# Outputs of the first layer's experts: stored by expert and gathered per token, or scattered to their tokens' rows and loaded

## The chip, the cores and the metric

The kernel runs on one core of a Trainium2 chip. A core has TensorE (PE; its weight loads are shown apart as PEld), VectorE (DVE), ScalarE (ACT), GpSimd (POOL) and SyncE (SP), and 16 DMA engines that all issuing engines share. The metric is the time of one execution in microseconds (us); of several executions the median is taken. All data are float32.

## The reference, cut to what matters

A graph transformer of two layers works on 3125 tokens with 256 numbers each. Layer 0 adds a graph attention and a linear attention to the tokens and then a mixture of eight experts, of which each token uses two. Layer 1 adds a graph convolution, another linear attention and eight dense experts.

```python
def _L0_ffn_ref(x, gate_w, gate_b, W1, b1, W2, b2):
    probs = softmax(xf @ gate_w + gate_b)
    top2_vals, top2_idx = top_k(probs, 2)
    cw = zeros((N, 8)).at[arange(N)[:, None], top2_idx].add(top2_vals)
    for w1, bb1, w2, bb2, we in zip(W1, b1, W2, b2, cw.T):
        h = gelu(xf @ w1 + bb1)
        y = h @ w2 + bb2
        acc = acc + we[:, None] * y
...
x = x + _L0_ffn_ref(_layernorm(x), ...)
xn = _layernorm(x)
x = x + _L1_gnn_ref(xn, edge_index, weight, bias) + _L1_mix_ref(xn, ...)
x = x + _L1_ffn_ref(_layernorm(x), ...)
```

## The kernel before

The tokens lie in 25 tiles of 128 rows (the last holds 53), resident as `X`. The experts of layer 0 take three steps.

*Dispatch* (`dispatch`, called for groups of up to four token tiles, interleaved with layer 0's other work). The tokens are normalised into `hd`, the gate's logits are compared, and each token gets two slots: an expert has 3328 slots in the table `tok` in device memory, filled in the order in which its tokens come. `slot` keeps the two slot numbers of each token (`slotF` as floats). GpSimd writes each token's normalised row to both slots with indirect transfers (L1172, two per token tile, 50 in all). `clear` has zeroed the table earlier, in layer 0's first part, so that unused slots read as zero rows.

*Expert tiles* (`tiles_of_experts`). A tile is 256 slots of one expert. Tiles 0 to 7 are the first of each expert; for the others `table_of_tiles`, made on DVE after the last dispatch, holds the expert and the row of each tile, and, since an output table `yex` is ordered by tile, new values of `slot` that point into `yex`. 28 tiles always run, four more stand in an `If` (L1412) that this input doesn't enter. SP loads per tile its rows (`hr`, L1354), two weights of 512 KB and a bias (`load`, rings of three). TensorE transposes `hr` (`turned`, copied by DVE to `hTe`), forms `mm` (four groups, gelu on ACT), then `acc`; DVE adds the bias into `yo` (L1394) and ACT's queue stores `yo` to `yex` as plain rows (L1395). Between the tiles SP also loads layer 1's dense experts (`fW`), three pieces of 256 KB after every third tile.

*Entry to layer 1.* The 25 token tiles go in seven groups (`ENT`: 2, 3, 4, 4, 4, 4, 4). `fetch_y` gathers for a group both outputs of each of its tokens from `yex` into `ye` (L1459, two indirect transfers per token tile, 50 in all; ring of three groups). `add_y` (L1463) adds them to `X` with their gates (L1469) and takes the mean and variance; the last tile of a group asks for the third group after it. `norm_y` normalises and transposes, `product_y` forms the rows that the graph convolution will gather and stores them group by group to `xtab` (L1498, SP), and `keys_values` forms keys and values of the linear attention. A loop (L1547 to L1562) takes the tiles in order, with the additions four tiles ahead and 18 of the 25 key steps inside. After it GpSimd gathers neighbours from `xtab` (L263), and pairs of layer 1 follow.

The order on each engine is set by the framework's scheduler; each engine runs its own list in order, and waits in front of an instruction hold up what stands behind it on that engine. Transfers go through three queues: SP's and ACT's (plain transfers), and GpSimd's (indirect ones).

Of the kernel before, what the change touches and what calls it, by code (L numbers as in the profile page):

```python
# [8 lines left out]
F32 = mybir.dt.float32  # L9
I32 = mybir.dt.int32  # L10
AF = mybir.ActivationFunctionType
ALU = mybir.AluOpType
AX = mybir.AxisListType

N, E, D = 3125, 50000, 256
P = 125
NT = N // P
# [5 lines left out]
NE = 8  # L23
# [32 lines left out]
def bc(ap, axis, n):  # L56

    a = ap.unsqueeze(axis)
    shape = list(a.shape)
    shape[axis] = n  # L60
    return a.to_broadcast(shape)
# [3 lines left out]
Q = 128  # L65
LAST = N - (NT - 1) * Q
NPAD = NT * Q
QB = 108
# [7 lines left out]
ME = 256  # L76
# [101 lines left out]
def fast_path(ctx: ExitStack, tc: tile.TileContext, i, out, ident, flag, X):  # L178
# [37 lines left out]
    def cols_of(name):  # L216
        return cols[:, _COLS[name][0]:_COLS[name][1]]
# [10 lines left out]
    def rows(t):  # L228
        return LAST if t == NT - 1 else Q
# [17 lines left out]
    def normed(dst, x, mv, rs, j):  # L247
        nc.vector.tensor_scalar(dst, x, mv[:, j, 0:1], rs[:, j:j + 1], op0=ALU.subtract, op1=ALU.mult)
# [78 lines left out]
    slotF = const.tile([Q, 2, NT], F32, name="slotF", tag="slotF")  # L327
    tok = dram.tile([NE * ST, D], F32, name="tok", tag="tok")
    yex = dram.tile([MT * ME, D], F32, name="yex", tag="yex")
    Mall = const.tile([Q, NCH, 4], F32, name="Mall", tag="Mall")  # L330
# [4 lines left out]
    with ExitStack() as l0:  # L335
# [14 lines left out]
        marks = dram.tile([QB * Q + NPAD, 4], F32, name="marks", tag="marks")  # L350
        zero = g0.tile([Q, Q], F32, name="zero", tag="zero")
        nc.vector.memset(zero, 0.0)
# [50 lines left out]
        def quads_of_edges():  # L403
# [23 lines left out]
            for k in range(8):  # L427
                a = k * SEGM
                if k:
# [6 lines left out]
            nc.gpsimd.dma_start(marks[0:QB * Q, :].rearrange("(p a r) c -> p a (r c)", p=QB, a=4),  # L436
                                bc(zero[0:QB, :], 1, 4))
            yield
# [231 lines left out]
        def clear(e):  # L670
            with queued():
                nc.vector.memset(zero, 0.0)
            nc.sync.dma_start(tok[e * ST:(e + 1) * ST, :].rearrange("(p r) (h c) -> p (r h) c", p=Q, h=2),
                              bc(zero, 1, 2 * ST // Q))
            if e == NE - 1:
                nc.sync.dma_start(xtab[NPAD:NPAD + 1, :].rearrange("o (h c) -> o h c", h=2), bc(zero[0:1, :], 1, 2))
                a = (MT - 4) * ME
                nc.sync.dma_start(yex[a:MT * ME, :].rearrange("(p r) (h c) -> p (r h) c", p=Q, h=2),
                                  bc(zero, 1, 8 * ME // Q))

# [435 lines left out]
        def dispatch(t0, n):  # L1116
# [3 lines left out]
            yield  # L1120
            hd = g0.tile([Q, 4, D], F32, name="hd", tag=f"m{t0 // 4 % 2}")
            pg = ps("seg", [Q, n, NE])
            for j in range(n):
                normed(hd[:, j, :], xs[:, j, :], mv, rs, j)
            yield
# [41 lines left out]
            nc.vector.tensor_reduce(sf[:, 1, :], sel, AX.X, ALU.max)  # L1167
            nc.vector.tensor_copy(slot[:, :, t0:t0 + n], sf)  # L1168
            for j in range(n):
                r = rows(t0 + j)  # L1170
                for k in range(2):
                    put = nc.gpsimd.indirect_dma_start(  # L1172
                        out=tok[:, :], out_offset=bass.IndirectOffsetOnAxis(ap=slot[0:r, k, t0 + j:t0 + j + 1], axis=0),
                        in_=hd[0:r, j, :], in_offset=None)
                    tc.add_to_no_dep_group("tok", put.ins)
                    tc.declare_no_dep(put.ins, group="tok", reason="no two tokens have the same row of an expert")
# [97 lines left out]
    with ExitStack() as l0e:  # L1274
# [6 lines left out]
        restI = ew.tile([Q, 1], I32, name="restI", tag="restI", bufs=1)  # L1281
        b1 = ew.tile([Q, MR, HB], F32, name="b1", tag="b1", bufs=1)
        be = cols_of("e_b1").rearrange("p (e f) -> p f e", f=HB)

        def table_of_tiles():

            def tmp(name, shape, dt=F32):
                return ew.tile([Q] + shape, dt, name=name, tag=name, bufs=1)
# [25 lines left out]
            nc.vector.tensor_tensor(pick, eoh, bc(start, 1, MR), ALU.mult)  # L1314
            row = tmp("row", [MR])
            nc.vector.tensor_reduce(row, pick, AX.X, ALU.add)
# [3 lines left out]
            for f in range(HB):  # L1320
                nc.vector.tensor_tensor(pick, eoh, bc(be[:, f, :], 1, MR), ALU.mult)
                nc.vector.tensor_reduce(b1[:, :, f], pick, AX.X, ALU.add)
            yield

            thr, off = tmp("thr", [NE, 2]), tmp("off", [NE, 2])
            nc.vector.tensor_copy(thr[:, :, 0], first)
            nc.vector.tensor_scalar(thr[:, :, 1], first, float(ME), None, op0=ALU.add)
            nc.vector.scalar_tensor_tensor(off[:, :, 0], eidx, -float(ME), first, op0=ALU.mult, op1=ALU.add)
            nc.vector.tensor_scalar(off[:, :, 1], start, float(ME - NE * ME), None, op0=ALU.add)
            inc = tmp("inc", [2 * NE])  # L1330
            off = off.rearrange("p e s -> p (e s)")
            nc.vector.tensor_copy(inc, off)
            nc.vector.tensor_tensor(inc[:, 1:2 * NE], off[:, 1:2 * NE], off[:, 0:2 * NE - 1], ALU.subtract)
            sp = tmp("sp", [2 * NT, 2 * NE])
            sl = slotF.rearrange("p k t -> p (k t)")
            nc.vector.tensor_tensor(sp, bc(sl, 2, 2 * NE), bc(thr.rearrange("p e s -> p (e s)"), 1, 2 * NT), ALU.is_ge)
            nc.vector.tensor_tensor(sp, sp, bc(inc, 1, 2 * NT), ALU.mult)
            back = tmp("back", [2 * NT])
            nc.vector.tensor_reduce(back, sp, AX.X, ALU.add)
            nc.vector.tensor_tensor(back, sl, back, ALU.subtract)  # L1340
            nc.vector.tensor_copy(slot.rearrange("p k t -> p (k t)"), back)
            yield

        def load(k):
# [3 lines left out]
            else:  # L1348
# [3 lines left out]
                src = tok[bass.ds(rr, ME), :]  # L1352
            hr = ew.tile([Q, 2, D], F32, name="hr", tag="hr", bufs=3)
            nc.sync.dma_start(hr, src.rearrange("(j p) c -> p j c", p=Q))  # L1354
# [19 lines left out]
        def tiles_of_experts(k0, k1):  # L1374
# [4 lines left out]
            for k in range(k0, k1):  # L1379
                w1, w2, _, b2 = loaded.pop(k)  # L1380
                gT = ew.tile([Q, HB, ME], F32, name="egT", tag="egT")
# [12 lines left out]
                nc.vector.tensor_tensor(yo, py, bc(b2, 1, 2), ALU.add)  # L1394
                nc.scalar.dma_start(yex[k * ME:(k + 1) * ME, :].rearrange("(j p) c -> p j c", p=Q), yo)  # L1395
                if k + 3 < k1:
# [55 lines left out]
    def fetch_y(g):  # L1452
        if g < len(ENT):
            t0, n = ENT[g]
            yes[g] = wk.tile([Q, 8, D], F32, name="ye", tag="gt1", bufs=3)
            for j in range(n):
                r = rows(t0 + j)
                for k in range(2):
                    nc.gpsimd.indirect_dma_start(  # L1459
                        out=yes[g][0:r, 2 * j + k, :], out_offset=None, in_=yex[:, :],  # L1460
                        in_offset=bass.IndirectOffsetOnAxis(ap=slot[0:r, k, t0 + j:t0 + j + 1], axis=0))

# [1017 lines left out]
```

## Time and profile before

| | |
|---|---|
| median of 5 executions | 2500.42 us (2498.88 to 2501.15) |
| profiled execution | 2501.07 us |
| its span | 2499.3 us |
| mean granted clock of TensorE | 0.963 |
| busy: PE, DVE, ACT, POOL | 2284.5, 1437.6, 1034.7, 1182.6 us |
| transfers | 229.92 MB, mean 92 GB/s |

The profile shows one execution. A line of it names the source line, the engine, the operation and the tiles as out<-in; the clock is the share of full speed that the throttle granted to TensorE. Where a helper issues the instructions, all have the helper's line (L260 for products, L263 for gathers), and are told apart by their tiles. "idle before, releaser" is the time in which the engine waited just before an instruction, and what ended the wait. A transfer has two times: that of its issue on a queue, and that until it has landed; the landing is known for a part of the transfers only.

Among the costliest groups, in busy us, are the gathers of layer 0 (L263 from `table`, 509.6) and of layer 1 (L263 from `xtab`, 436.8), both on POOL, the products of the dense and other experts on PE, and, each about 50 us on POOL, the gathers of L1459 and the scatters of L1172.

### The profile page before, as it was taken

To read this page: it belongs to the slowest core of one execution; us is meant where nothing else is said; L and a number is where in the kernel's file an instruction comes from. 1 tells how busy PE (TensorE), PEld (TensorE's weight loads), DVE (VectorE), ACT (ScalarE), POOL (GpSimd) and SP (SyncE) were. 2 spreads that over 40 slices of the span, in tenths; PEclk is the share of its full clock that TensorE was granted. 3 is DMA by queue.
4 is the path that set the end of the run, shared out by engine and by line. 5 is a ranking of instruction groups with operands and counts; after the bars stand their busy time and mean duration, and the time that the engine had idled before them with its cause. 6 is when DMAs were issued, how large, how long until landed. Compare 5 with 4: busy or idle time off the path is not lost. (4 is left out here: it accounts for less than half of the span.)

```text
span 2499.3 us, 27694 instructions
## 1 busy us (share of the span) xinstructions
PE 2284.5 (91%) x9288; PEld 1628.4 (65%) x9288; DVE 1437.6 (58%) x3426; ACT 1034.7 (41%) x2012; POOL 1182.6 (47%) x1250
## 2 busy tenths in 40 slices
PE   3886799999999989999899699969799999999998
PEld 3664567776677856778566588846466665656665
DVE  3475656887778977689544621247555554444331
ACT  2724235635447364383654322236243333333332
POOL 2445776726677347630022300043666766767700
PEclk8998999999999999999999799989799999999999
DMA  7103132413234131120111388622322333333300
GB/s 223 38 12 91 46 84 54 127 56 103 64 104 130 37 104 50 48 66 13 37 60 60 119 292 287 225 94 80 93 84 86 106 91 101 100 92 99 102 13 8
DMA packets 187748, 229.92 MB, mean 92 GB/s; under 512 B 25743, under 2 KB 153527, under 8 KB 187595
## 3 DMA queue, kind: packets, MB, share of 16 engines
q0 software_dynamic: 45184, 106.92, 15.0%
q1 hardware_dynamic: 131557, 111.19, 14.2%
q10 hardware_dynamic: 10854, 9.92, 1.3%
q8 instruction: 77, 1.26, 0.2%
q14 instruction: 76, 0.62, 0.1%
HBM read 169.27 MB, written 58.67 MB: 91 GB/s over the span
## 5 line engine op out<-in xcount | busy, mean ns | idle before, releaser
L263 POOL DMA_INDIRECT gt<-table,srcI x432 | 509.6, 1180 | 210.6 <-issue 119.5
L263 POOL DMA_INDIRECT gt<-xtab,src x432 | 436.8, 1011 | 224.8 <-issue 109.7
L260 PE MATMUL mm<-hT,w 128*128 128x512 f32 (+3 forms) x896 | 365.0, 546 | 7.7 <-ACT gT L975 5.1
L260 PE MATMUL acc<-w,gT 128*128 128x256 f32 (+1 forms) x1600 | 365.9, 384 | 0.1
L260 PEld LDWEIGHTS acc<-w,gT 128*128 128x128 f32 (+1 forms) x1600 | 298.6, 189 | 48.8 <-issue 3.4
L1662 ACT ACTIVATE fh<-mm,bn_b,bn_s 128x512 f32<-128x512 f32 (+2 forms) x224 | 162.0, 723 | 349.0 <-PE mm L260 348.9
L975 ACT ACTIVATE gT<-mm,cols 128x512 f32<-128x512 f32 (+3 forms) x224 | 139.8, 632 | 268.1 <-PE mm L260 266.0
L260 PEld LDWEIGHTS mm<-hT,w 128*128 128x128 f32 x896 | 163.8, 192 | 132.9 <-issue 87.2
L316 DVE SCALAR_TENSOR_TENSOR X<-acc,rw,X 128x256 f32<-128x256 f32 x200 | 94.9, 482 | 217.3 <-PE acc L260 216.9
L260 PE MATMUL mm<-wqkv,hT 128*128 128x256 f32 x800 | 205.6, 391 | 8.5 <-ACT K L849 5.3
L260 PE MATMUL acc<-fw_f_Wo,fh 128*128 128x256 f32 (+1 forms) x800 | 197.7, 385 | 0.5 <-DVE X L316 0.3
L260 PE MATMUL mm<-fh,fw_f_W 128*128 128x512 f32 (+2 forms) x448 | 187.9, 549 | 2.1
L260 PE MATMUL mm<-xc,fw_f_W 128*128 128x512 f32 (+2 forms) x448 | 185.1, 543 | 0.0
L260 PEld LDWEIGHTS acc<-fw_f_Wo,fh 128*128 128x128 f32 (+1 forms) x800 | 142.8, 187 | 54.9 <-ACT fh L1662 12.0
L260 PEld LDWEIGHTS mm<-wqkv,hT 128*128 128x128 f32 x800 | 143.7, 194 | 32.8 <-ACT K L849 9.1
L1459 POOL DMA_INDIRECT ye<-yex,slot x50 | 50.7, 1013 | 239.3 <-DVE oh L270 224.3
L260 PEld LDWEIGHTS mm<-fh,fw_f_W 128*128 128x128 f32 x448 | 81.1, 189 | 87.7 <-issue 39.9
L729 DVE TENSOR_TENSOR vals<-m,w 128x2080 f32<-128x2080 f32 x54 | 124.9, 2313 | 19.0 <-ACT w L724 18.9
L260 PEld LDWEIGHTS mm<-xc,fw_f_W 128*128 128x128 f32 x448 | 85.0, 192 | 58.5 <-issue 40.0
L260 PE MATMUL acc<-M,qT 128*128 128x256 f32 x400 | 105.1, 407 | 12.8 <-ACT qT L945 10.5
L263 POOL DMA_INDIRECT es<-etab,at x54 | 59.8, 1108 | 119.3 <-DVE at L374 98.9
L1172 POOL DMA_INDIRECT tok<-hd,slot x50 | 50.2, 1005 | 125.3 <-DVE slot L1168 86.5
(464 smaller groups left out, 3868.0 us busy)
## 6 DMA issues: line engine op xcount, KB each, us to landing
ew<-in_e_W SPq DMA_DIRECT2D x56, 512.0 KB, 4.7
tok<-zero SPq DMA_DIRECT2D x8, 3328.0 KB, 14.0
w<-in_W SPq DMA_DIRECT2D x8, 1024.0 KB, 11.5
hr<-tok SPq DMA_DIRECT2D x28, 256.0 KB, 5.3
yex<-yo ACTq DMA_DIRECT2D x28, 256.0 KB, 5.1
gt<-table,srcI POOLq DMA_INDIRECT x432, 2.5
gt<-xtab,src POOLq DMA_INDIRECT x432, 2.8
fw_f_W<-in_f_W SPq DMA_DIRECT2D x16, 256.0 KB, 2.7
```

The lines of the kernel that those rows point to most:

```text
L260: nc.tensor.matmul(pm, a, b, start=(k == 0), stop=(k == len(lhs) - 1))
L263: nc.gpsimd.indirect_dma_start(out=dst, out_offset=None, in_=tab[:, :], in_offset=bass.IndirectOffsetOnAxis(ap=idx[:, b:b + 1], axis=0))
L316: nc.vector.scalar_tensor_tensor(X[0:r, t, :], py, cw, X[0:r, t, :], op0=ALU.mult, op1=ALU.add)
L729: nc.vector.tensor_tensor(v.rearrange("p j (h f) -> p j h f", f=65), bc(m[:, h0 - b0:h0 - b0 + k, 4:69], 2, 4), bc(w[:, h0 - b0:h0 - b0 + ...
L975: nc.scalar.activation(gT[:, f, 0:w], pm, AF.Gelu, bias=col("b1", l * NF + f))
L1172: put = nc.gpsimd.indirect_dma_start(out=tok[:, :], out_offset=bass.IndirectOffsetOnAxis(ap=slot[0:r, k, t0 + j:t0 + j + 1], axis=0), in_= ...
L1459: nc.gpsimd.indirect_dma_start(out=yes[g][0:r, 2 * j + k, :], out_offset=None, in_=yex[:, :], in_offset=bass.IndirectOffsetOnAxis(ap=slot[ ...
L1662: nc.scalar.activation(hn[:, a, 0:w], pm, AF.Relu, bias=bn[s][1][:, c:c + 1], scale=bn[s][0][:, c:c + 1])
```

## The change

A row of `tok` gets two numbers more: the token's number plus one, and its first slot plus a constant `NONE`, both written into `hd` at dispatch. An expert tile thus knows for each of its rows whose token it holds, and whether this is the token's first or second slot. From that DVE makes a row number of a new table `y2`: the first outputs of all tokens in order, then the second ones, then rows of their own for empty slots. GpSimd scatters the tile's two halves there, instead of the plain store on ACT's queue. `fetch_y` becomes two plain loads per group on SP, one for the first outputs and one for the second (a third piece where the last tile has 53 rows). The part of `table_of_tiles` that turned slots into rows of `yex`, and the clearing of `yex`, are gone.

```diff
@@ -325,8 +325,11 @@
     first = const.tile([Q, NE], F32, name="first", tag="first")
     nc.gpsimd.iota(first, pattern=[[ST, NE]], base=0, channel_multiplier=0, allow_small_or_imprecise_dtypes=True)
     slotF = const.tile([Q, 2, NT], F32, name="slotF", tag="slotF")
-    tok = dram.tile([NE * ST, D], F32, name="tok", tag="tok")
-    yex = dram.tile([MT * ME, D], F32, name="yex", tag="yex")
+
+    tok = dram.tile([NE * ST, D + 2], F32, name="tok", tag="tok")
+
+    NONE = 2 * NPAD + 1
+    y2 = dram.tile([3 * NPAD + NE * ST, D], F32, name="y2", tag="y2")
     Mall = const.tile([Q, NCH, 4], F32, name="Mall", tag="Mall")
     closed = {}
     xtab = dram.tile([NPAD + 1, D], F32, name="xtab", tag="xtab")
@@ -348,7 +351,7 @@
         SEGM = 24 * SEG
         etab = dram.tile([8 * SEGM], F32, name="etab", tag="etab")
         marks = dram.tile([QB * Q + NPAD, 4], F32, name="marks", tag="marks")
-        zero = g0.tile([Q, Q], F32, name="zero", tag="zero")
+        zero = g0.tile([Q, Q + 1], F32, name="zero", tag="zero")
         nc.vector.memset(zero, 0.0)
         oks = const.tile([Q, 8], F32, name="oks", tag="oks")
         nc.vector.memset(oks, 1.0)
@@ -434,7 +437,7 @@
                 a += 3 * W * (P1 - q)
                 nc.gpsimd.dma_start(etab[a:(k + 1) * SEGM].rearrange("(p j) -> p j", p=1), zero[0:1, 0:(k + 1) * SEGM - a])
             nc.gpsimd.dma_start(marks[0:QB * Q, :].rearrange("(p a r) c -> p a (r c)", p=QB, a=4),
-                                bc(zero[0:QB, :], 1, 4))
+                                bc(zero[0:QB, 0:Q], 1, 4))
             yield
             bF = tmp("bF", [RB], tag="vs", p=1)
             nc.vector.tensor_copy(bF, bI)
@@ -670,13 +673,11 @@
         def clear(e):
             with queued():
                 nc.vector.memset(zero, 0.0)
-            nc.sync.dma_start(tok[e * ST:(e + 1) * ST, :].rearrange("(p r) (h c) -> p (r h) c", p=Q, h=2),
-                              bc(zero, 1, 2 * ST // Q))
+            n = ST // Q * (D + 2) // (Q + 1)
+            nc.sync.dma_start(tok[e * ST:(e + 1) * ST, :].rearrange("(p r) c -> p (r c)", p=Q)
+                              .rearrange("p (n c) -> p n c", n=n), bc(zero, 1, n))
             if e == NE - 1:
-                nc.sync.dma_start(xtab[NPAD:NPAD + 1, :].rearrange("o (h c) -> o h c", h=2), bc(zero[0:1, :], 1, 2))
-                a = (MT - 4) * ME
-                nc.sync.dma_start(yex[a:MT * ME, :].rearrange("(p r) (h c) -> p (r h) c", p=Q, h=2),
-                                  bc(zero, 1, 8 * ME // Q))
+                nc.sync.dma_start(xtab[NPAD:NPAD + 1, :].rearrange("o (h c) -> o h c", h=2), bc(zero[0:1, 0:Q], 1, 2))
 
         m2 = []
 
@@ -1118,10 +1119,12 @@
             xs = X[:, t0:t0 + n, :]
             mv, rs = ln_stats(xs, n)
             yield
-            hd = g0.tile([Q, 4, D], F32, name="hd", tag=f"m{t0 // 4 % 2}")
+            hd = g0.tile([Q, 4, D + 2], F32, name="hd", tag=f"m{t0 // 4 % 2}")
+            nc.gpsimd.iota(hd[:, 0:n, D], pattern=[[Q, n]], base=t0 * Q + 1, channel_multiplier=1,
+                           allow_small_or_imprecise_dtypes=True)
             pg = ps("seg", [Q, n, NE])
             for j in range(n):
-                normed(hd[:, j, :], xs[:, j, :], mv, rs, j)
+                normed(hd[:, j, 0:D], xs[:, j, :], mv, rs, j)
             yield
             for j in range(n):
                 pt = transposed(hd[:, j, :])
@@ -1166,6 +1169,7 @@
             nc.vector.tensor_tensor(sel, took, at, ALU.mult)
             nc.vector.tensor_reduce(sf[:, 1, :], sel, AX.X, ALU.max)
             nc.vector.tensor_copy(slot[:, :, t0:t0 + n], sf)
+            nc.vector.tensor_scalar(hd[:, 0:n, D + 1], sf[:, 0, :], float(NONE), None, op0=ALU.add)
             for j in range(n):
                 r = rows(t0 + j)
                 for k in range(2):
@@ -1280,6 +1284,9 @@
         rowI = ew.tile([Q, MR], I32, name="rowI", tag="rowI", bufs=1)
         restI = ew.tile([Q, 1], I32, name="restI", tag="restI", bufs=1)
         b1 = ew.tile([Q, MR, HB], F32, name="b1", tag="b1", bufs=1)
+        rowF = ew.tile([Q, MR], F32, name="rowF", tag="rowF", bufs=1)
+        nth2 = ew.tile([Q, 2], F32, name="nth2", tag="nth2", bufs=1)
+        nc.gpsimd.iota(nth2, pattern=[[Q, 2]], base=0, channel_multiplier=1, allow_small_or_imprecise_dtypes=True)
         be = cols_of("e_b1").rearrange("p (e f) -> p f e", f=HB)
 
         def table_of_tiles():
@@ -1312,7 +1319,7 @@
             nc.vector.scalar_tensor_tensor(start, tiles, -float(ME), first, op0=ALU.mult, op1=ALU.add)
             pick = tmp("pick", [MR, NE])
             nc.vector.tensor_tensor(pick, eoh, bc(start, 1, MR), ALU.mult)
-            row = tmp("row", [MR])
+            row = rowF
             nc.vector.tensor_reduce(row, pick, AX.X, ALU.add)
             nc.vector.scalar_tensor_tensor(row, nth, float(ME), row, op0=ALU.mult, op1=ALU.add)
             nc.vector.tensor_scalar(row, row, float(ME), float(NE * ST - ME), op0=ALU.add, op1=ALU.min)
@@ -1320,25 +1327,6 @@
             for f in range(HB):
                 nc.vector.tensor_tensor(pick, eoh, bc(be[:, f, :], 1, MR), ALU.mult)
                 nc.vector.tensor_reduce(b1[:, :, f], pick, AX.X, ALU.add)
-            yield
-
-            thr, off = tmp("thr", [NE, 2]), tmp("off", [NE, 2])
-            nc.vector.tensor_copy(thr[:, :, 0], first)
-            nc.vector.tensor_scalar(thr[:, :, 1], first, float(ME), None, op0=ALU.add)
-            nc.vector.scalar_tensor_tensor(off[:, :, 0], eidx, -float(ME), first, op0=ALU.mult, op1=ALU.add)
-            nc.vector.tensor_scalar(off[:, :, 1], start, float(ME - NE * ME), None, op0=ALU.add)
-            inc = tmp("inc", [2 * NE])
-            off = off.rearrange("p e s -> p (e s)")
-            nc.vector.tensor_copy(inc, off)
-            nc.vector.tensor_tensor(inc[:, 1:2 * NE], off[:, 1:2 * NE], off[:, 0:2 * NE - 1], ALU.subtract)
-            sp = tmp("sp", [2 * NT, 2 * NE])
-            sl = slotF.rearrange("p k t -> p (k t)")
-            nc.vector.tensor_tensor(sp, bc(sl, 2, 2 * NE), bc(thr.rearrange("p e s -> p (e s)"), 1, 2 * NT), ALU.is_ge)
-            nc.vector.tensor_tensor(sp, sp, bc(inc, 1, 2 * NT), ALU.mult)
-            back = tmp("back", [2 * NT])
-            nc.vector.tensor_reduce(back, sp, AX.X, ALU.add)
-            nc.vector.tensor_tensor(back, sl, back, ALU.subtract)
-            nc.vector.tensor_copy(slot.rearrange("p k t -> p (k t)"), back)
             yield
 
         def load(k):
@@ -1350,7 +1338,7 @@
                 rr = nc.values_load(rowI[0:1, k - NE:k - NE + 1], engines=(SPE,), min_val=0, max_val=NE * ST - ME)
                 v1, v2, v3 = (i[n][bass.ds(re, 1)] for n in ("e_W1", "e_W2", "e_b2"))
                 src = tok[bass.ds(rr, ME), :]
-            hr = ew.tile([Q, 2, D], F32, name="hr", tag="hr", bufs=3)
+            hr = ew.tile([Q, 2, D + 2], F32, name="hr", tag="hr", bufs=3)
             nc.sync.dma_start(hr, src.rearrange("(j p) c -> p j c", p=Q))
             w1 = ew.tile([Q, KC, EH], F32, name="ew1", tag="ew1", bufs=3)
             nc.sync.dma_start(w1, v1.rearrange("o (k p) c -> p (o k) c", p=Q))
@@ -1377,7 +1365,19 @@
             loaded = {k: load(k) for k in range(k0, min(k0 + 3, k1))}
             hT = turned(loaded[k0][2])
             for k in range(k0, k1):
-                w1, w2, _, b2 = loaded.pop(k)
+                w1, w2, hr, b2 = loaded.pop(k)
+
+                to, toI = (ew.tile([Q, 2, 2] if dt is F32 else [Q, 2], dt, name=f"to{dt is I32}", tag=f"to{dt is I32}",
+                                   bufs=3) for dt in (F32, I32))
+                own = ew.tile([Q, 2], F32, name="own", tag="own", bufs=3)
+                if k < NE:
+                    nc.vector.tensor_scalar(own, nth2, float(k * ST + NONE), None, op0=ALU.add)
+                else:
+                    nc.vector.tensor_scalar(own, nth2, rowF[:, k - NE:k - NE + 1], float(NONE), op0=ALU.add, op1=ALU.add)
+                nc.vector.tensor_tensor(to[:, 0], hr[:, :, D + 1], own, ALU.is_equal)
+                nc.vector.scalar_tensor_tensor(to[:, 0], to[:, 0], -float(NPAD), hr[:, :, D], op0=ALU.mult, op1=ALU.add)
+                nc.vector.scalar_tensor_tensor(to[:, 1], hr[:, :, D], 0.0, own, op0=ALU.is_equal, op1=ALU.mult)
+                nc.vector.scalar_tensor_tensor(toI, to[:, 0], float(NPAD - 1), to[:, 1], op0=ALU.add, op1=ALU.add)
                 gT = ew.tile([Q, HB, ME], F32, name="egT", tag="egT")
                 for f in range(HB):
                     pm = ps("mm", [Q, ME])
@@ -1392,7 +1392,12 @@
                             [w2[:, f, :] for f in range(HB)])
                 yo = ew.tile([Q, 2, D], F32, name="yo", tag="yo", bufs=3)
                 nc.vector.tensor_tensor(yo, py, bc(b2, 1, 2), ALU.add)
-                nc.scalar.dma_start(yex[k * ME:(k + 1) * ME, :].rearrange("(j p) c -> p j c", p=Q), yo)
+                for j in range(2):
+                    put = nc.gpsimd.indirect_dma_start(
+                        out=y2[:, :], out_offset=bass.IndirectOffsetOnAxis(ap=toI[:, j:j + 1], axis=0),
+                        in_=yo[:, j, :], in_offset=None)
+                    tc.add_to_no_dep_group("y2", put.ins)
+                    tc.declare_no_dep(put.ins, group="y2", reason="no two rows go to the same row")
                 if k + 3 < k1:
                     loaded[k + 3] = load(k + 3)
                 if k0:
@@ -1453,12 +1458,8 @@
         if g < len(ENT):
             t0, n = ENT[g]
             yes[g] = wk.tile([Q, 8, D], F32, name="ye", tag="gt1", bufs=3)
-            for j in range(n):
-                r = rows(t0 + j)
-                for k in range(2):
-                    nc.gpsimd.indirect_dma_start(
-                        out=yes[g][0:r, 2 * j + k, :], out_offset=None, in_=yex[:, :],
-                        in_offset=bass.IndirectOffsetOnAxis(ap=slot[0:r, k, t0 + j:t0 + j + 1], axis=0))
+            for k in range(2):
+                node_dma(nc.sync, yes[g][:, k:2 * n:2, :], y2[k * NPAD:(k + 1) * NPAD, :], t0, n)
 
     def add_y(t):
```

`node_dma` moves rows of consecutive token tiles with one transfer, and the last, shorter tile with another.

## The prediction

> **What bounds the kernel now.** I read the busy shares first (TensorE 91%, so most of the span can't be shortened from outside it), then the stretches around the edit as windows, then what ended the waits there, then one expert tile as a timeline. Windows, columns: us, then busy us and instructions of PE, PEld, DVE, ACT, POOL, granted clock, DMA share, GB/s:
>
> ```profile
> 1410.00:1430.00 20.00, 3.97 (x16) 3.31 (x16) 10.39 (x70) 2.24 (x4) 11.33 (x12) 0.50 0.65 231
> 1430.00:1450.00 20.00, 16.74 (x70) 13.78 (x71) 12.29 (x46) 6.79 (x12) 0.00 (x0) 0.77 0.80 257
> 1450.00:1540.00 90.00, 90.00 (x436) 78.72 (x436) 18.70 (x30) 22.71 (x49) 0.00 (x0) 1.00 0.91 300
> 1540.00:1640.00 100.00, 99.97 (x491) 87.02 (x490) 20.34 (x35) 25.62 (x54) 0.00 (x0) 1.00 0.64 212
> 1640.00:1664.00 24.00, 4.41 (x21) 3.54 (x19) 8.12 (x24) 2.68 (x5) 11.40 (x12) 0.65 0.23 72
> 1664.00:1720.00 56.00, 45.71 (x178) 29.49 (x178) 43.39 (x131) 35.14 (x89) 39.26 (x38) 0.93 0.40 120
> 1720.00:1755.00 35.00, 34.53 (x138) 23.78 (x139) 24.95 (x46) 20.49 (x54) 0.00 (x0) 0.92 0.13 45
> ```
>
> The expert stage (1435 to 1644) is TensorE alone; the DMA engines are 91% busy until 1540, while layer 1's weights are loaded too, and 64% after. TensorE loses time at the stage's two ends. At the second end it is the 50 gathers ye<-yex. Tile ye (duration min/median/max, first and last start), then pieces of the chain of waits (start, us):
>
> ```profile
> L1459 POOL DMA_INDIRECT ye<-yex,slot x50: 942/947/1580, 1649.0 to 1713.1; - x50
>   DVE X L1469: 20.7, 19
> DMA to landing us min/median/max: 2.6/2.8/6.0
> ```
>
> ```profile
> 1711.17 5.95 DMA ye<-yex,slot
> 1717.55 0.47 DVE X L1469
> ```
>
> From 1649.0 to 1714 POOL issues one gather each 1.25 us; DVE waits for their landing 19 times, 20.7 us. TensorE stands from 1644.4 to 1664.5, at 1667.8 to 1671.2 and for most of 1711 to 1720. Now one expert tile (start, us; T is the end of acc), and landings of transfers in 1450 to 1600 and, for the scatters, in 1405 to 1450:
>
> ```profile
> 1562.75 1.89 PE L260 MATMUL mm<-hTe,ew 128*128 128x256 f32 x8
> 1562.95 0.69 DVE L1394 TENSOR_TENSOR yo<-acc,eb 128x512 f32<-128x512 f32 x1 [2.77 <-PE acc L260]
> 1563.67 0.42 ACTq L1395 DMA_DIRECT2D yex<-yo  x1
> 1564.24 0.37 SPq L1354 DMA_DIRECT2D hr<-tok  x1
> 1566.86 0.69 DVE L1369 COPY hTe<-tr 128x512 f32<-128x512 f32 x1 [3.22 <-PE tr L1367]
> 1570.11 1.24 PE L260 MATMUL mm<-hTe,ew 128*128 128x256 f32 x5
> ```
>
> ```profile
> yex<-yo ACTq DMA_DIRECT2D x20, 256.0 KB, 6.0
> hr<-tok SPq DMA_DIRECT2D x18, 256.0 KB, 6.0
> ```
>
> ```profile
> tok<-hd,slot POOLq DMA_INDIRECT x12, 6.8
> ```
>
> The period is 1570.11-1562.75 = 7.36 us, all TensorE. yo starts at T+0.2, the store at T+0.9, hr at T+1.5. Single store landings: 6.68, 6.21, 5.73, 6.53 up to 1535 (mean 6.29), 4.99 to 5.05 after, 2.12 with the queues empty at 1630; hr 7.33, 6.04, 5.97, later 5.17 and 5.07.
>
> **The change, part by part.** *Entry to layer 1 (gain).* The 50 gathers go; plain loads on SP, two per group, take their place. The last scatter leaves at about 1646.5 (last yo 1644.44 + 0.69, two pitches of 1.27 as the tok scatters have: 0.97 + 0.30), and lands 2.4 to 2.8 later (fastest tok scatter, median gather): 1649.2. SP passes the If as now (1648.1), so loads start near 1650. A first group of 512 KB lands in 3.5 (hr needs 3.06 to 3.28 for 256 KB at 1440): 1653.5 against 1655.7 now, the second at 1655.5 against 1662.8. DVE then needs about 7 us for four tiles' additions and statistics, so TensorE starts at 1661.6, 2.9 earlier. From there TensorE has 25 tiles x 1.08 us (tr 0.22, seg 0.86) + 18 key steps x 2.61 (1.72 + 0.45 + 0.44) = 74 us, which take 86.6 now (1664.5 to 1751.1) with the waits for gathers in them. DVE has 76 us of work in the same stretch, so not all of 12.6 comes back; I take 92% efficiency, 80 us. End 1741.6: **gain 9.5**. Ends: 6 if DVE's order costs what the gathers cost (only the start and half of the waits of 1667 and 1711), 13 if TensorE runs at 77 us. It carries through: the last product feeds xtab, and layer 1's gathers start at 1755.35, released by DVE va, with pairs and TensorE after them.
>
> *Expert stage (loss).* Per tile, POOL issues two scatters (56 x 0.97 us on an engine that is at 0.00 here) in place of one store on ACT's queue (28 x 0.42). DVE gets five small operations (its smallest rows here take 0.1 to 0.17 us): 0.7 of the some 6 of 7.4 us that it is idle. Costed at nothing by themselves; if DVE had no room they would be 28 x 0.7 = 20. The waits are what costs. The order of DVE in the changed kernel is yo(k), toI(k+3), hTe(k+2), to(k+4), yo(k+1). toI has three buffers, so toI(k+3) waits until both scatters of tile k have landed, and hTe(k+2), which TensorE wants at T+7.36, stands behind it. With L from the second scatter's issue (T+2.3) to its landing, hTe(k+2) is there at T + 2.3 + L + 0.25 + 0.69 + 0.05 = T+3.3+L: a stall when L > 4.05. Lower end of L: 2.8, a gather's median in 1649 to 1717 at 40% DMA share: no stall. If the scatters land when the store did: L = 3.6 (5.0+0.9-2.3) after 1540, no stall; 4.9 before, 0.83 a tile. Upper end 6.8, the tok scatters in a crowd: 2.7 a tile. Crowded tiles: 13 (T from 1441 to 1537). A scatter carries half a store's bytes and meets the same weight loads, and each tile that stalls thins the load, so I take a third of 0.83 x 13 = 11: **loss 3.5**, ends 0 and 13 x 2.7 = 36. Also behind: to(k+4) waits for hr(k+4), issued at T+1.5; at 6.0 to 7.3 us it lands at T+7.5 to 8.8, and yo(k+1) (due T+7.56) waits with it, by at most 1.7; this meets the same crowded tiles and I count it in the same ends.
>
> *Start of the stage (loss).* One iota per dispatch (the iotas here take 0.13 to 0.16 us) and one more in front of the last four tok scatters, with a pitch: 0.3. hTe(0), copied at 1433.84, gets to(0) and part of to(1) ahead of it, the latter waiting for hr(1): 0.9. **Loss 1.2**, ends 0.5 and 2.
>
> *At nothing.* Eleven DVE operations of the tile table go (three near 1 us): DVE is idle 80% of the stage that hides them, and were it full, that would be 5 us gained. Rows two numbers wider (1032 for 1024 bytes, 0.8% of 7 MB) and the clears of layer 0 lie under its TensorE work; uncovered, 0.2 us. On SP the y2 loads wait for add_y and stand in front of xtab stores, which nothing reads before 1755; uncovered, one store of some 4 us.
>
> Sum: -9.5 + 3.5 + 1.2 = -4.8. Of the profiled execution (2501.07, of which 1.8 lie outside the span of 2499.3) that leaves 2496.3; the median of the runs, 2500.42, lies 0.65 below it, so 2495.6: **2495**, rounded to the gain's side.
>
> One row speaks for scatters that don't suffer under DVE: the gathers' issues stay at 947 ns median although DVE is busy 43 of 56 us around them. The Trainium skill (SBUF — State Buffer, section "SBUF: two separate sides") warns of the opposite: a transfer issued from GpSimd can't get its descriptors written while VectorE runs a two-port copy, and should then go by ScalarE's or SyncE's queue. By that rule the 50 gathers' removal would bring more and the 56 scatters would each lag by up to one 0.69 us copy, 0.7 a tile on L; no row here shows such a lag. The same skill (DMA: Bandwidth & Descriptors, section "Issuing engines are not separate DMA queues") says that all queues share the 16 engines and interleave; by it the scatters land no sooner than the store did, 0.83 x 13 = 11 us of stall, and the sum would be about 2503.
>
> **The rivals.**
> *R1, the two cancel.* The scatters land as the store did in the crowd; stall 5 to 12, sum -4 to +4: about 2500. For it: the store's landings of 5.7 to 6.7. Against it: half the bytes each, and the first is under way 1.27 us earlier.
> *R2, slower: toI's wait holds up DVE's queue.* One mechanism: DVE at toI, behind it hTe, behind that TensorE. It decides when the stall passes 8.3 us in all, or L > 4.7 over 13 tiles. With L = 5.3 to 5.8 (the store's delay under load, 4.2 us, halved for each scatter and added to 2.4, plus the first one's rest) and hr's lateness, 1.25 to 1.7 a tile, 16 to 22: 2500.4 - 8.3 + 19 = 2511. For it: 6.8 for the tok scatters. Against: those come twelve in a row at 1.27.
> *R3, the gathers were only half the entry's bound.* DVE's 76 us set it; gain 5, other terms as above: 2500. For it: DVE is 78% busy there. Against: 20.7 us of DVE's waits are on ye.
>
> **How the numbers follow.** Below 0.2%, 5 us, a measurement of this kernel can't tell a change. Forecast (small stall) 0.40, R1 and R3 together 0.23, R2 0.37. The forecast's own range is 2488 to 2500; the signs are shared, so 8 in 10 needs the way to R2: 2487 (gain 13, no stall) to 2514 (R2 with its upper per-tile cost). Faster 0.40, same 0.23, slower 0.37.
>
> **What would show it.** Right: no ye in what ends DVE's waits, TensorE idle from 1644 for 17 us, last seg of the entry near 1742 by the old clock, xtab gathers 9 earlier. The stall: DVE toI waiting for y2 at length, TensorE mm waiting for hTe in tiles before 1540, period above 7.36. What would make it wrong: periods of 8.5 and more there, or an entry still over 86 us.

## The result, and the profile after

The changed kernel takes 2504.97 us (median of 32 executions, 2499.87 to 2513.68) against 2500.98 for the kernel before, measured beside it; the ratio is 1.0016 (95% interval 1.001 to 1.0022). A second measurement (e5_after, below) gave 1.0020 (1.0011 to 1.0029). So it is slower by 4 us. That is less than the 0.2% that the prediction took for the smallest change to be told, but both intervals lie above 1, on the other side of no change than the forecast.

Behind the small difference stand two large ones. The windows of the changed kernel, with the stretches moved to where its stages lie (columns as before: us, busy us and instructions of PE, PEld, DVE, ACT, POOL, clock, DMA share, GB/s):

```profile
1450.00:1550.00 100.00, 90.76 (x421) 76.45 (x420) 22.12 (x75) 22.78 (x48) 23.30 (x24) 0.97 0.80 262
1550.00:1671.00 121.00, 115.47 (x550) 97.33 (x548) 27.43 (x101) 29.75 (x61) 29.20 (x30) 0.99 0.60 194
1671.00:1688.00 17.00, 0.29 (x2) 0.00 (x0) 6.99 (x24) 0.62 (x2) 1.94 (x2) 0.66 0.58 183
1688.00:1763.00 75.00, 74.62 (x314) 51.23 (x315) 66.70 (x176) 54.63 (x141) 0.00 (x0) 0.96 0.28 92
```

The expert stage, where TensorE was busy 190 of 190 us, has holes now: 9 us in its first 100 and 5.5 in the rest. It also lost clock. The windows from the first to the last addition of the bias (yo) and of a stretch right behind the longest hole, then the products that ran there:

```profile
1450.60:1671.30 220.70, 205.92 (x966) 173.24 (x965) 49.55 (x176) 52.53 (x109) 52.50 (x54) 0.98 0.69 224
1499.70:1506.40 6.70, 6.68 (x18) 5.39 (x19) 1.12 (x6) 1.42 (x3) 1.94 (x2) 0.55 0.40 136
```

```profile
1499.72 6.66 PE L260 MATMUL mm<-hTe,ew 128*128 128x256 f32 x16 [3.99 <-DVE hTe L1357]
```

Of the stage's 220.7 us TensorE stands for 14.8, and for the same products it is busy 205.9 us, where it was busy 198.6 before, with a granted clock of 1.00 throughout. Sixteen products that take 3.75 us elsewhere took 6.66 here.

The entry to layer 1 has lost its holes: once TensorE starts, it is busy 74.6 of 75 us. The tile views say why. The row numbers toI (shown as toTrue), with the scatters that read them; then the loads that took the gathers' place:

```profile
L1396 POOL DMA_INDIRECT y<-yo,toTrue x56: 967/972/1021, 1451.6 to 1673.6; - x56
L1380 DVE SCALAR_TENSOR_TENSOR toTrue<-toFalse x28: 149/160/161, 1439.3 to 1655.8; 128x2 int32<-128x2 f32 x28
...
who waited for it (us, times):
  DVE toTrue L1380: 144.5, 24
...
DMA to landing us min/median/max: 2.4/4.6/7.6
```

```profile
L174 SPq DMA_DIRECT2D ye<-y x16: 345/466/1616, 1677.6 to 1703.3; - x16
...
  DVE X L1470: 3.7, 2
...
DMA to landing us min/median/max: 3.6/5.5/6.1
```

DVE waits 24 times, 144.5 us, for scatters to land, in front of an operation of 0.16 us. At the entry its 19 waits for gathers (20.7 us) have become 2 waits for loads (3.7 us).

The following table is read from the instructions' start times in four profiles, two executions of each kernel (us):

| stretch | before | after |
|---|---|---|
| start to the first of the last 12 token scatters | 1409.6, 1406.7 | 1412.5, 1412.9 |
| from there to the first yo | 36.2, 37.3 | 38.1, 38.4 |
| first yo to last yo (27 expert tiles) | 198.6, 198.4 | 220.7, 220.6 |
| last yo to the first xtab gather | 110.9, 109.7 | 93.1, 93.3 |
| from there to the end | 744.0, 747.6 | 742.9, 743.6 |

The expert stage costs 22 us more, the entry 16 to 18 less, and 5 to 7 us more are spent ahead of the first yo. Both profiled executions of the changed kernel lie some 4 us above the median of its runs (2509.11 the first), so the spans differ by 8 to 9 where the medians differ by 4.

### The profile page after: what moved, and what is told of

It reads as the page before. It is cut to its first block, busy times and chain, and to the rows that moved or that the text cites. A ratio compares the mean times of both kernels' runs of the same rounds, so it can differ in the third digit from the quotient of the medians.

```text
span 2507.4 us, 27867 instructions
## 1 busy us (share of the span) xinstructions
PE 2287.3 (91%) x9288; PEld 1627.3 (65%) x9288; DVE 1444.6 (58%) x3562; ACT 1034.0 (41%) x2012; POOL 1187.0 (47%) x1264
## 5 line engine op out<-in xcount | busy, mean ns | idle before, releaser
L263 POOL DMA_INDIRECT gt<-xtab,src x432 | 435.3, 1008 | 274.7 <-issue 109.7
L1396 POOL DMA_INDIRECT y<-yo,toTrue x56 | 54.4, 972 | 189.7 <-DVE yo L1394 167.2
L260 PE MATMUL mm<-hTe,ew 128*128 128x256 f32 x448 | 109.8, 400 | 15.2 <-DVE hTe L1357 15.2
```

The costliest lines, as they stand in the source:

```text
L260: nc.tensor.matmul(pm, a, b, start=(k == 0), stop=(k == len(lhs) - 1))
L263: nc.gpsimd.indirect_dma_start(out=dst, out_offset=None, in_=tab[:, :], in_offset=bass.IndirectOffsetOnAxis(ap=idx[:, b:b + 1], axis=0))
L1396: put = nc.gpsimd.indirect_dma_start(out=y2[:, :], out_offset=bass.IndirectOffsetOnAxis(ap=toI[:, j:j + 1], axis=0), in_=yo[:, j, :], in_o ...
```

## The experiments

Two theories of the lost 22 us. *A*: toI has three buffers, so toI(k+3) waits on DVE until tile k's scatters have landed, and hTe(k+2), which TensorE needs, stands behind it. *B*: the scatters crowd the DMA engines, and TensorE would wait for weights and rows whatever DVE does.

The first four kernels ran on a chip that needed some 10% more for every kernel (2767.02 us for the kernel before), without the changed kernel beside them; they are compared with each other, and by the length of their stages.

**Eight buffers of toI** (e1_ring8):

```diff
-                                   bufs=3) for dt in (F32, I32))
+                                   bufs=3 if dt is F32 else 8) for dt in (F32, I32))
```

> The changed kernel with eight buffers of toI in place of three, so that DVE writes the row numbers of a tile long before the scatters of the tile before it have landed. Theory A (toI's wait holds up DVE's list, behind it hTe, behind that TensorE): the 27 periods from the first yo to the last go from 220.7 back to 199 to 204 us, DVE's 144.5 us of waits for the scatters vanish, and the time is 2505 less 17 to 22, 2483 to 2488. Theory B (the scatters crowd the DMA engines, and TensorE would wait for weights and rows whatever DVE does): the stage stays above 214 us, with waits for ew or hr in place of those for hTe, and the time is 2499 or more.

Measured: 2713.44 us, 0.9794 of before (0.975 to 0.9838); stage 198.4 us, and no toI waits for a scatter any more. The two kernels of the first four with three buffers (e2_early, e4_gather) have stages of 222.1 and 221.1. That is theory A.

**The iota of nth2 at the kernel's start** (e2_early):

```diff
+    nth2 = const.tile([Q, 2], F32, name="nth2", tag="nth2")
+    nc.gpsimd.iota(nth2, pattern=[[Q, 2]], base=0, ...)
...
-        nth2 = ew.tile([Q, 2], F32, name="nth2", tag="nth2", bufs=1)
-        nc.gpsimd.iota(nth2, pattern=[[Q, 2]], base=0, ...)
```

> The changed kernel with the iota of nth2 made at the kernel's start and not between the token scatters. Theory: DVE's first own waits 5.1 us for that iota, which stands on POOL behind eight token scatters, and the slots of the last two token tiles stand behind own on DVE; without it the last four scatters follow the others at the pitch of 1.27 (they start at 1422.95 and not 1425.64 in the profile's time), and the time falls by 2.7, to 2502. Rival: the last four are late through the extra operations of the dispatch itself, or TensorE's start is set by the weights anyway; then nothing changes beyond 1 us, 2504 to 2505.5.

The wait that it is about, in the changed kernel: DVE's waits of 1410 to 1430 (us, times, longest), and the POOL rows there (start, us):

```profile
DVE own L1374 <- POOL nth L1289: 5.1, 1, 5.1
```

```profile
1421.68 0.97 POOL L1176 DMA_INDIRECT tok<-hd,slot  x1 [0.30 <-issue]
1422.66 0.16 POOL L1289 IOTA nth<- 128x2 f32 x1
1425.64 0.99 POOL L1176 DMA_INDIRECT tok<-hd,slot  x1 [2.82 <-issue]
```

Measured: 2740.38 us, 0.9896 of before (0.9847 to 0.9944). The last 12 token scatters take 14.3 us from first to last, 16.9 in e1_ring8 and in the changed kernel, 14.1 before: the part of the theory on POOL holds. Its worth in time can't be read from this run alone, the changed kernel not having run beside it.

**Both** (e3_both):

> Eight buffers of toI and the early iota together. If the two are independent, the sum: 2505 - 20 - 2.7 = 2482, range 2480 to 2486. If the start's lateness is made good inside the expert stage, as much as with the eight buffers alone, 2483 to 2488. Theory B of the ring's run: 2496 or more.

Measured: 2714.27 us, 0.9805 of before (0.9761 to 0.9849), no faster than the eight buffers alone. TensorE's first expert product comes 12.8 us after the last token scatter here, 11.9 in e1_ring8: part of the 2.6 us is lost again before TensorE starts, and of the rest the runs, which spread by 27 us, show nothing.

**The gathers back at the entry** (e4_gather), with all else as changed. Two rows of zeros that the table needs cost two small transfers.

```diff
+    at2 = lp.tile([Q, 2, NT], I32, name="at2", tag="at2")
+    nc.gpsimd.iota(at2, pattern=[[NPAD, 2], [Q, NT]], base=0, channel_multiplier=1)
...
-            for k in range(2):
-                node_dma(nc.sync, yes[g][:, k:2 * n:2, :], y2[k * NPAD:(k + 1) * NPAD, :], t0, n)
+            for j in range(n):
+                r = rows(t0 + j)
+                for k in range(2):
+                    nc.gpsimd.indirect_dma_start(
+                        out=yes[g][0:r, 2 * j + k, :], out_offset=None, in_=y2[0:2 * NPAD, :],
+                        in_offset=bass.IndirectOffsetOnAxis(ap=at2[0:r, k, t0 + j:t0 + j + 1], axis=0))
```

> The changed kernel with the 50 indirect gathers back at the entry to layer 1, now from y2 by the tokens' numbers; scatters, rings and the expert stage as in the changed kernel (two small clears of unused rows are added). It undoes the gain alone. If the entry's gain is the 17.8 us that the two profiles show (from the last yo to the first gather of xtab, 110.9 against 93.2): 2505 + 17.8 = 2523, range 2519 to 2527. If the gain is the 9.5 that was worked out, and the rest of the 17.8 came from something else (the later end of the expert stage, a different clock): 2514. If DVE's own work sets the entry: 2510 or less.

Measured: 2780.87 us, 1.0033 of before (0.9999 to 1.0068), 40 more than e2_early, with the entry at 138.1 us against 92.9 there. It was run again on a chip that needs 2503.71 for the kernel before (e11_gather2):

> The gathers back at the entry to layer 1, as in the first call, on a chip that runs before in 2500, it is hoped. The entry's gain alone undone: from the last yo to the first xtab gather 110 to 113 us in place of 93, and 2505.5 + 17 = 2522, range 2519 to 2527, so 1.007 to 1.010 of before. If gathers from y2 by the tokens' order are slower than those from yex (138.1 us on the slow chip): 2530 or more.

Measured: 2530.71 us, 1.0113 of before (1.0096 to 1.0131). That is 27.0 us above the kernel before beside it, where the changed kernel (e5_after) is 4.1 above its own: 22.9 us; entry 114.0 us. DVE's waits at the gathers are back, as in the kernel before (20.7 us, 19 times):

```profile
L1469 POOL DMA_INDIRECT ye<-y,at x50: 945/949/1579, 1683.8 to 1748.1; - x50
...
  DVE X L1479: 20.6, 18
```

The gathers are worth 114.0 - 93.3 = 20.7 us of entry, more than the 17 expected. Here they also begin later: the first one at 1683.8, 7.3 us after the last yo (1676.5), against 4.6 before; it follows an operation of DVE (oh) that waited 6.0 us for the scatters, the last of them issued at 1678.7. Of the other 2 us some lie in the expert stage, which takes 222.6 us in this profile; why isn't known.

**The same on a chip like the first** (e5_after: the changed kernel itself, e6_both2: e3_both once more, beside each other)

> The changed kernel itself beside the kernel before, since the chip of the first four runs ran all kernels some 10% longer (before: 2767 us) and the changed kernel was not among them. On a chip like the first: ratio 1.001 to 1.002, stage 219 to 223 us from the first yo to the last, entry (last yo to first xtab gather) 92 to 94. On the slow chip, if the two halves weigh as they did: stage 222 as in the runs with three buffers, entry 93, and before + 0 to 5 us; if its runs of three buffers are what the early iota's run showed (27 us faster than before), the entry weighs more there.

> Eight buffers of toI and the early iota once more, in one call with the changed kernel. Theory A: faster than the changed kernel by 20 to 25 us, stage 198 to 200 us. On a chip where before takes 2500: 2480 to 2486, ratio to before 0.992 to 0.994. If it is less than 15 us faster than the changed kernel, the stage's gain is given back later.

and, for a second profile of the kernel before on that chip (e9_before, given in the table above):

> The kernel before, for a profile on this chip: stage 198 to 200 us, entry 110 to 112 us if the chip is like the first; on the slow chip the entry with its 50 gathers is longer, 125 to 140 (the gathers from y2 took 138.1 there), and that is why the early iota's run gained 27 us there.

Measured: e9_before 2501.34 us with a stage of 198.4 and an entry of 109.7; e5_after 2505.79 us, 1.0020 of before (1.0011 to 1.0029). e6_both2 2480.84 us, **0.9922 of before (0.9909 to 0.9936)**, 25 us less than the changed kernel. Its windows of the expert stage:

```profile
1450.00:1550.00 100.00, 100.00 (x487) 86.22 (x486) 25.99 (x82) 26.20 (x56) 26.67 (x28) 1.00 0.91 298
1550.00:1650.00 100.00, 99.76 (x489) 85.86 (x486) 25.83 (x87) 26.20 (x54) 25.75 (x27) 1.00 0.60 198
```

TensorE is full again, at a granted clock of 1.00 and at the same DMA share of 0.91 as before, with the same 56 scatters on POOL. So neither the scatters' bytes nor their issue cost anything there, and the lower clock went with the holes. DVE's waits in 1450 to 1650 of e6_both2, and the largest of the changed kernel in 1450 to 1671 (us, times, longest):

```profile
DVE hTe L1357 <- PE tr L1355: 55.0, 22, 3.2
DVE toFalse L1377 <- DMA hr<-tok: 52.6, 21, 4.9
DVE yo L1394 <- PE acc L260: 33.9, 16, 6.2
```

```profile
DVE toTrue L1380 <- DMA y<-yo,toTrue: 144.5, 24, 9.8
```

In e6_both2 DVE waits for TensorE and for hr, and no longer for scatters. The wait for hr, which the prediction named as a second loop, is real (52.6 us), but costs the stage nothing: it takes 198.4 us.

**Layer 1's weights spread over the tiles** (e8_spread), with three buffers of toI:

```diff
-                if k >= 5 and k % 3 == 2 and (k - 5) // 3 < NE:
-                    e = (k - 5) // 3
-                    for w, name in zip(fW, ("f_W1", "f_W2", "f_Wo")):
-                        nc.sync.dma_start(w[:, e], ...)
+                if k >= 4:
+                    e = (k - 4) // 3
+                    w, name = list(zip(fW, ("f_W1", "f_W2", "f_Wo")))[(k - 4) % 3]
+                    nc.sync.dma_start(w[:, e], ...)
```

> The changed kernel (three buffers of toI) with layer 1's expert weights loaded one piece of 256 KB after every tile from tile 4 on, in place of three pieces after every third tile; the bytes are the same. If the scatters land late because three pieces stand in front of them at once, their longest landings fall from 7.6 to below 5.5 us and the stage's 220.7 us to 205 to 213; the time falls by 8 to 15. If the mean load counts and not the burst, the long periods (9 to 11 us every third tile) are only evened out to about 8 and the stage stays at 217 to 223, the time within 4 us of the changed kernel's.

Measured: 2505.75 us, 1.0017 of before (1.0002 to 1.0031), and 2505.79 for the changed kernel beside it. The stage takes 217.9 us, against 220.6 beside it: the second of the two expectations. The median landing is 4.6 us, as with the burst. Nor can the longest period be put down to the burst: it is 10.15 us without it, and 11.59 and 10.08 in the two profiles of the changed kernel.

**Clearing the token table in other pieces** (e10_clear512), on top of e3_both. This run is about a step that the prediction had costed at nothing:

```diff
-            n = ST // Q * (D + 2) // (Q + 1)
-            nc.sync.dma_start(tok[...].rearrange("(p r) c -> p (r c)", p=Q)
-                              .rearrange("p (n c) -> p n c", n=n), bc(zero, 1, n))
+            n = ST // Q * (D + 2) // Q
+            flat = tok[...].rearrange("(p r) c -> p (r c)", p=Q)
+            nc.sync.dma_start(flat[:, 0:n * Q].rearrange("p (n c) -> p n c", n=n), bc(zero[:, 0:Q], 1, n))
+            nc.sync.dma_start(flat[:, n * Q:], zero[:, 0:ST // Q * (D + 2) - n * Q])
```

> The version with eight buffers and the early iota, and the table tok cleared in pieces of 512 bytes with a short rest per partition, in place of pieces of 516 bytes. Theory: the 516-byte pieces are what makes a clear take 27.3 us in place of 14.0 with nearly the same bytes, and the loads behind it on SP's queue late; that costs 2.4 us between the first and the last gather of layer 0 (879.9 us against 877.2). Then the clears land in 14 to 16 us, that stretch goes back to 877 to 878, and the time is 2478 to 2480. Rival: the rows of 1032 bytes or the order of the transfers make the difference; the clears stay above 20 us and nothing changes, 2480 to 2483.

Measured: 2483.97 us, 0.9918 of before (0.9905 to 0.9931), the same as e6_both2. The clears land after 20 to 21 us, between the two; each rest of 208 bytes per partition holds SP's queue for 13 to 18 us, and the stretch of layer 0 isn't shorter (881.3 us). The run doesn't settle what the clears cost.

## Why the prediction was wrong, and where it was right

*Entry to layer 1, "gain 9.5": right in its mechanism, too small.* Measured 17.8 and 16.4. The start was right: 2.9 earlier was expected, and TensorE's idle time after the last tile goes from 20.1 to 17.0 us. The step that was mis-sized is "I take 92% efficiency, 80 us". The 25 tiles and 18 key steps, worked out at 74 us, took 74.3, from 1688.3 to 1762.7. Also, the 86.6 us set against them end at 1751.1 with the last seg, when 17 key steps are done; to the same point the changed kernel takes 71.7 us (to 1760.05), not 80. DVE's 76 us were no reason for a discount: 7 us of them lie ahead of TensorE's first product, and 66.7 beside its 75 us. Rival R3, the gathers as only half the bound, falls with it: putting them back costs 20.7 us.

*Expert stage, "loss 3.5": right chain, wrong size; this is the step that turned the sign.* Measured 22.1. The prediction had hTe(k+2) at T+3.3+L, a stall beyond L = 4.05, and then took "a third of 0.83 x 13". The chain is as it was described. Here is one tile of the changed kernel (start, us):

```profile
1525.41 0.69 DVE L1394 TENSOR_TENSOR yo<-acc,eb 128x512 f32<-128x512 f32 x1
...
1527.66 0.97 POOL L1396 DMA_INDIRECT y<-yo,toTrue  x1 [0.30 <-issue]
...
1534.03 0.16 DVE L1380 SCALAR_TENSOR_TENSOR toTrue<-toFalse 128x2 int32<-128x2 f32 x1 [7.93 <-DMA y<-yo,toTrue]
1534.11 0.68 DVE L1357 COPY hTe<-tr 128x512 f32<-128x512 f32 x1
...
1534.85 3.75 PE L260 MATMUL mm<-hTe,ew 128*128 128x256 f32 x16 [2.10 <-DVE hTe L1357]
1535.10 0.68 DVE L1394 TENSOR_TENSOR yo<-acc,eb 128x512 f32<-128x512 f32 x1
```

From the second scatter's issue to toI are L = 1534.03-1527.66 = 6.4 us; 3.3 + 6.4 = 9.7, and the period is 1535.10-1525.41 = 9.69. Likewise L = 5.9 gives 9.2 (9.16), 5.6 gives 8.9 (8.88), 5.0 gives 8.3 (8.30), 8.3 gives 11.6 (11.59). What was wrong is what was put in for L, and what was left out. In the 13 tiles that were called crowded L is 5.0 us in the mean, nearly the 4.9 of scatters that land when the store did. So the step that failed is the cut to a third, for "half a store's bytes" and a thinner load. The seven known landings of single scatters there are 3.72 to 7.60 us, with a median of 4.87, against 5.73 to 6.68 for the stores; but the second scatter is issued 2.24 us after the start of yo, where the store was issued after 0.73, so on average nothing was won. And the mean isn't enough: L goes from 3.5 to 8.3, what is above the threshold costs time, and what is below gives none back. These 13 tiles lost 15.8 us. The other 6.3 were lost after them, where no stall was expected: three of the long periods (9.52, 9.08 and 9.50) come after 1580, and at the first of them the second scatter itself was issued late, 3.6 us after yo in place of 2.24.

A part of both is a term that the sum doesn't have: the granted clock. The period of 10.33 us behind the longest hole has L = 3.7, so no stall of its own, but a mean clock of 0.72; the one of 9.08 at 1593 has L = 5.0, which would make 8.3, and a clock of 0.81. Together they are 4.7 us longer than the 7.37 of a full tile. The second profile of the changed kernel has two such tiles as well (9.47 us at 0.82, 9.08 at 0.81); the kernel before and e6_both2 have none. Which holes bring the clock down isn't settled: one of 2.1 us (1532.8 to 1534.9) did not.

Rival R2 had the mechanism, with L = 5.3 to 5.8 in each of the 13 tiles and 16 to 22 us. That 22.1 were measured is in part luck: R2 had neither the clock nor the tiles after 1580.

*Start of the stage, "loss 1.2": 1.9 and 1.1 in the two pairs up to the first yo, but not by its parts.* The iota "in front of the last four tok scatters" was priced at 0.3 on POOL. It cost some 2.7 there, since DVE's own waited 5.1 us for it and the slots of the last tokens stood behind own: a wait that was added and whose queue wasn't followed. Taking it away gave no measurable time, though: up to the first yo that stretch takes 37.7 us in e3_both and 38.4 in e1_ring8, and the executions of each spread by 27 us.

*"At nothing".* No stretch shows a gain from the removed table operations, and the y2 loads hold DVE up only twice, 3.7 us. The clears of layer 0 were put under TensorE's work; between the first and the last gather from the layer's table they stand beside 2.2 to 3.1 us more (876.8 and 877.6 before, 879.9 and 879.8 after). That they cause it is argued, not shown.

*The sum.* -9.5 + 3.5 + 1.2 was to be -4.8. Measured in the first pair of profiles: -17.8 at the entry, +22.1 in the stage, +1.9 at its start, +2.9 ahead of it, -1.1 after. The outcome looks like rival R1 (the two cancel), with each side about twice as large as R1 had it: R2's stall against a relief that no case had. The rule cited on queues that share the DMA engines (the Trainium skill, DMA: Bandwidth & Descriptors, section "Issuing engines are not separate DMA queues") pointed the right way: from it the prediction drew that scatters on another queue land no sooner than the store, L = 4.9, and the mean L of the 13 tiles is 5.0. The other rule cited (SBUF — State Buffer, section "SBUF: two separate sides") finds no support here: the 56 scatters' issues take 967 to 1021 ns, and where L was longest, 8.3 us, DVE stood idle from before that scatter's issue until it had landed (9.8 us), so that no copy on DVE can have held it up.

## What to carry to other kernels

In this kernel a small tile that a transfer reads was free again only when the transfer had *landed*: the operation that overwrites it waited 144.5 us in all, and what stood behind it on the same engine waited too. So count a ring's depth in landing times under the load of that stage, not in tiles: five more buffers of eight bytes per partition (with the early iota, whose own worth the runs did not show) turned 4 us of loss into 21 of gain. How few more would do was not tried.

When a change of many parts moves the time little, time its stages separately before looking for a small cause.

Where a period has no slack, put the threshold beside the rows of the landing time and carry their spread through the sum, tile by tile: at a threshold of 4.05 and rows from 2.8 to 6.8, one value in the middle was no forecast, and the largest, with 36 us, would have been too much. A hole can also cost more than its length: here the two tiles at a lowered clock were together 4.7 us longer than full ones.

## What the runs showed of the hardware

The clears, 3328 KB in pieces of 512 bytes before, 3354 KB in pieces of 516 after, have nearly the same number of packets (6810 and 6807 on their queue) and take about twice the time (14.3 and 27.1 us). Queue q1 (SP) and the issues, first of e9_before (the kernel before, profiled again) at 784 to 812 us, then of e6_both2 at 790 to 818:

```profile
q1 hardware_dynamic: 6810, 3.54, 43.9%
...
tok<-zero SPq DMA_DIRECT2D x1, 3328.0 KB, 14.3
gt<-table,srcI POOLq DMA_INDIRECT x14, 3.9
```

```profile
q1 hardware_dynamic: 6807, 3.56, 85.8%
...
tok<-zero SPq DMA_DIRECT2D x1, 3354.0 KB, 27.1
gt<-table,srcI POOLq DMA_INDIRECT x14, 7.2
```

The packets' time on the DMA engines doubles (43.9% to 85.8% of 28 us), and the gathers beside them land after 7.2 us in place of 3.9. Over 200 to 1000 us the DMA share rises from 0.29 to 0.44 at nearly the same 81 and 80 GB/s. Whether the length of a piece counts or where it starts (rows of 1032 bytes, so hardly a piece starts at a round address) stays open: 512-byte pieces in the same rows still took some 20 us.
